# Turned rows of the routing reused by the shared layers, from SBUF or by way of DRAM

## The chip, the cores and the metric

The kernel runs on one core of a Trainium2 chip. Its time is the device time of an execution in microseconds; of several runs the median counts, and of a range the lowest and the highest are given. One further execution is profiled; from it come the trace and all times of single instructions. PE is the matmul engine, PEld its loading of the stationary operand, DVE, ACT and POOL are the vector, scalar and GpSimd engines, and SP is the engine that issues most transfers. Each of them runs its own instructions in order.

## The reference

The input is x, 16 batches of 128 tokens with 256 features in float32, and a context of the same shape. Four layers follow each other, each with a layer normalisation `ln` in front and a gate behind:

```python
x = x + tanh(g_xattn[0]) * long_conv(ctx, ctx, ln(x))
x = x + tanh(g_ffn[0]) * (shared_swiglu(ln(x)) + experts8_top2(ln(x)))
x = x + tanh(g_xattn[1]) * causal_attention16(ln(x), ctx, ctx)
x = x + tanh(g_ffn[1]) * (shared_relu2(ln(x)) + experts32_top6(ln(x)))
```

Both mixtures of experts have a router, which picks 2 of 8 or 6 of 32 experts for every token, and a shared layer, which every token passes. The router and the shared layer of one mixture take the same normalised rows. The shared layer has 1024 hidden units with `silu(g) * u` in the first mixture and 256 with squared ReLU in the second.

## The kernel before, in words

**Tiles.** x stays in SBUF as 16 tiles `xs[b]` of 128 tokens by 256 features, to which every layer adds its part. The layers work on chunks of batches: `CHUNKS` is (0,4), (4,8), (8,12), (12,14), (14,16), and the routing of the second mixture on `GROUPS` (0,4), (4,8), (8,12), (12,14), (14,15), (15,16). A matmul needs its rows with the features on the partitions. So the rows of a chunk are normalised and turned: `stats` (L161 to L182) gives mean and reciprocal deviation, and `turned` (L189 to L208) normalises each tile on DVE (L202), transposes its two halves on PE into a PSUM bank (L205) and copies the bank, two tiles at a time, into a tile `xT` on ACT (L207). In a profile all uses of it share these lines and differ by the names: tp_f and row for the routing, tp_s and xn_s for the shared layers, tp_at and xn_at for the attention. Tiles `xT` come from a ring of four (tag "xT", bufs=4), the PSUM banks for transposes ("tr") from a ring of two.

**First mixture.** `sends0(i)` (L701) does the routing of one half of the batches: norm (statistics, the rows as they are to be sent, and their transposes), choose (logits lg_r at L382, then the selection on DVE), place (each row's place in its expert's list) and the sends (L716), indirect DMAs on POOL that scatter rows into a DRAM buffer. `tiles0` (L736 to L793) reads them back by tiles of 128 rows of one expert (the loads `got`, L747), multiplies, and stores the results `parts`; `combine0` gathers them. `shared0(c)` (L630 to L683) is the shared layer of chunk c as a list of steps: turn, eight times hidden(j) with the matmuls pg and pu (L608, in `up`) and hs (L424), with back(j) (os, L660) one step behind, and add.

**Second half.** `attend` (L814 to L904) is the attention of one batch in five steps, with keys and values loaded by SP (L822, L823). `dispatch(g)` (L934 to L980) is the routing of a group for the second mixture with norm, choose, place and sends (L963); its masks are mb (L550), its positions pos (L555 to L559), its destinations dst (L600). `shared1` (L907 to L930) is the shared layer of a group: turn, two matmul steps p (L608) and o_sh (L616). The expert stage then reads all sent rows (`got`, L1161), turns them (xt, L1175), and runs through 114 tiles of experts.

**What sets the order.** Steps are closures in lists. `woven` (L1012) spreads several lists evenly against each other. `with_sums0` (L1028) makes the list of a chunk's shared layer that is woven with the attention. For the last batches the order is written out by hand (L1063 to L1080), and `some(n)` takes the next n steps of `shared1` there. A scheduler then moves instructions of each engine within what dependencies allow, so that the order of an engine can differ from that of the program. SP's transfers take turns on eight hardware semaphores.

**Where the same rows are turned twice.** The routing's norm in `sends0` and `dispatch` keeps mean and deviation (`keep=True`); `shared0` and `shared1` use them later to normalise and turn the same rows of x again, by `chunk_T` (L369) or `turned`:

```python
        def turn():
            got["xT"] = chunk_T(c, "s0", norm=norm)
...
        def turn():
            got["xT"] = xT = work.tile([P, KC, TOK], F32, tag="xT", name=f"xTs_{g}", bufs=4)
            turned(work, list(range(b0, b1)), mv, rs, columns(xT, b1 - b0), f"s1{g}")
```

Of the kernel before, what the change touches and what calls it, by code (L numbers as in the profile page):

```python
# [10 lines left out]
F32 = mybir.dt.float32  # L11
# [7 lines left out]
P = 128  # L19
B = 16  # L20
D = 256
KC = D // P
# [10 lines left out]
WARM = 22  # L33

E0, SH0, TOPK0 = 8, 8, 2
PARTS0 = [(0, 8), (8, 16)]
NT0 = 8 * TOPK0 + E0 - 1
W0_ROW = 3 * D
# [15 lines left out]
def flamingo(ctx: ExitStack, tc: tile.TileContext, a: dict, out: bass.AP):  # L54
# [154 lines left out]
    def columns(xT, n):  # L209
        return lambda j: xT[:, :, 2 * j * P : min(2 * j + 2, n) * P].rearrange("p c (k t) -> p k c t", t=P)  # L210
# [158 lines left out]
    def chunk_T(c, label, scale=1.0, norm=None):  # L369
        xT = work.tile([P, KC, TOK], F32, tag="xT", name=f"xT_{label}{c}", bufs=4)  # L370
        tiles = list(range(*CHUNKS[c]))
        mv, rs = norm or stats(tiles, f"{label}{c}")
        turned(work, tiles, mv, rs, columns(xT, len(tiles)), f"{label}{c}", scale=scale)
        return xT


    def router(xT, n, rw, ne, label):

# [248 lines left out]

        return [[(b - b0, b) for b in range(i, min(i + 2, b1))] for i in range(b0, b1, 2)]

    def shared0(c, norm):  # L630

        b0, b1 = CHUNKS[c]
        n = (b1 - b0) * P
        tiles = pairs(b0, b1)
        got, hs = {}, [None] * SH0

        def turn():
            got["xT"] = chunk_T(c, "s0", norm=norm)

        def hidden(j):  # L640
            cols = slice(j * P, (j + 1) * P)
            p1 = up(lambda kc: wB[:, kc, 0, cols], got["xT"], n, f"pg_{c}_{j}")
            p2 = up(lambda kc: wB[:, kc, 1, cols], got["xT"], n, f"pu_{c}_{j}")
            hs[j] = work.tile([P, TOK], F32, tag="h", name=f"hs{c}_{j}", bufs=3)[:, :n]
            silu_gate(p1, p2, hs[j], n, f"{c}_{j}")

        def back(j):
            if j == 0:
                got["o"] = [bank("so", f"os{c}_{i}", 2) for i in range(len(tiles))]
                for o in got["o"]:  # L650
                    T.matmul(
                        o.rearrange("p (h t) -> p h t", t=P),
                        lhsT=zeros_b,
                        rhs=ident_b.unsqueeze(1).to_broadcast([P, 4, P]),
                        start=True,
                        stop=False,
                    )
            for o, ts in zip(got["o"], tiles):
                for k, (t, _) in enumerate(ts):
                    T.matmul(  # L660
                        o[:, k * D : (k + 1) * D],
                        lhsT=hs[j][:, t * P : (t + 1) * P],
                        rhs=wC[:, j, :],
                        start=False,
                        stop=(j == SH0 - 1 and k == len(ts) - 1),
                    )

        def add():
            for o, ts in zip(got["o"], tiles):
                for k, (_, b) in enumerate(ts):  # L670
                    V.scalar_tensor_tensor(xs[b], o[:, k * D : (k + 1) * D], tg_h, xs[b], ALU.mult, ALU.add)

        def step(j):
            if j < SH0:
                hidden(j)
            if j > 0:
                back(j - 1)

        return [turn] + [lambda j=j: step(j) for j in range(SH0 + 1)] + [add]
# [4 lines left out]
            follow(ins, other, reason)  # L684


    norms0 = {}

    def sends0(i):

        b0, b1 = PARTS0[i]
        chunks = [c for c in range(len(CHUNKS)) if b0 <= CHUNKS[c][0] < b1]
        got = {}
        scatters = []

        def norm(c):
            n = CHUNKS[c][1] - CHUNKS[c][0]
            tiles = list(range(*CHUNKS[c]))
            rows = [work.tile([P, ROW], F32, tag="row", name=f"row0_{b}", bufs=8) for b in tiles]
            got.setdefault("rows", []).extend(rows)  # L700
            got["xT"] = xT = work.tile([P, KC, TOK], F32, tag="xT", name=f"xT_f0{c}", bufs=4)  # L701
            norms0[c] = stats(tiles, f"f0{c}", keep=True)
            turned(work, tiles, *norms0[c], columns(xT, n), f"f0{c}", keep=lambda k: rows[k][:, :D])

        def choose(c):
            if c == chunks[0]:
                got["masks"] = small.tile([P, HALF, E0], BF16, tag="masks0", name=f"masks0_{i}", bufs=1)
                got["eqs"] = small.tile([P, HALF, TOPK0, E0], F32, tag="eqs0", name=f"eqs0_{i}", bufs=1)
            choose0(got["xT"], c, got["masks"], got["eqs"])

        def place():
            got["table"] = place0(i, got["masks"], got["eqs"])

        def send(t):
            for k in range(TOPK0):
                ins = G.indirect_dma_start(  # L716
                    out=sent0[i][:, :],
                    out_offset=bass.IndirectOffsetOnAxis(ap=places0[:, b0 + t, k : k + 1], axis=0),
                    in_=got["rows"][t][:, :D],
                    in_offset=None,  # L720
                )
                for other in scatters:
                    tc.declare_no_dep(ins.ins, other.ins, reason="no two of the rows sent share a place")
                scatters.append(ins)
                if k == 0:
                    paced(ins)

        steps = []
        for c in chunks:
            steps += [lambda c=c: norm(c), lambda c=c: choose(c)]  # L730
        return steps + [place] + [lambda t=t: send(t) for t in range(b1 - b0)], got, scatters
# [172 lines left out]
        return [lambda: scores(0), lambda: scores(1), turn, values, add]  # L904


    def shared1(mv, rs, g):  # L907

        b0, b1 = GROUPS[g]
        n = (b1 - b0) * P  # L910
        got, hs = {}, []

        def turn():
            got["xT"] = xT = work.tile([P, KC, TOK], F32, tag="xT", name=f"xTs_{g}", bufs=4)
            turned(work, list(range(b0, b1)), mv, rs, columns(xT, b1 - b0), f"s1{g}")

        def hidden(j):
            ps = up(lambda kc: ws[:, j, kc * P : (kc + 1) * P], got["xT"], n, f"p1_{g}_{j}")
            r = work.tile([P, TOK], F32, tag="act", name=f"relu_{g}_{j}", bufs=4)[:, :n]
            S.activation(r, ps, AF.Relu)  # L920
            h = work.tile([P, TOK], F32, tag="h", name=f"h1_{g}_{j}", bufs=3)[:, :n]
            S.activation(h, r, AF.Square)
            hs.append(h)

        def back(i, ts):
            down(hs, [ws[:, j, KC * P :] for j in range(SH1)], lambda t: tg_f[:, 1:2], ts, f"sh{g}_{i}")

        return (
            [turn]
            + [lambda j=j: hidden(j) for j in range(SH1)]  # L930
            + [lambda i=i, ts=ts: back(i, ts) for i, ts in enumerate(pairs(b0, b1))]
        )
# [3 lines left out]
    def dispatch(g):  # L936
# [5 lines left out]
        def norm():  # L942
            got["rows"] = rows = [
                work.tile([P, ROW], F32, tag="row", name=f"row{b}", bufs=8) for b in range(b0, b1)
            ]
            got["xT"] = xT = work.tile([P, KC, TOK], F32, tag="xT", name=f"xT1_{g}", bufs=4)
            tiles = list(range(b0, b1))
            got["norm"] = stats(tiles, f"f1{g}", keep=True)
            turned(work, tiles, *got["norm"], columns(xT, n), f"f1{g}", keep=lambda k: rows[k][:, :D])

        def choose():
            got["chosen"] = choose1(got["xT"], g)
# [23 lines left out]
        sends = []  # L976
        for t in range(n):
            sends += [lambda t=t: send(t), *wait[1:]]
        shares[g] = lambda: shared1(*got["norm"], g)
        return [norm, *wait[1:], choose, *wait, place, *sends]  # L980

    aT, begun = {}, {}
# [32 lines left out]
    def woven(*lists):  # L1015

        at = [((i + 0.5) / len(l), k, step) for k, l in enumerate(lists) for i, step in enumerate(l)]
        for _, _, step in sorted(at, key=lambda x: x[:2]):
            step()
# [5 lines left out]
    def sums0(c):  # L1025
        return [lambda b=b: combine0(b) for b in range(*CHUNKS[c])]

    def with_sums0(c):  # L1028

        steps = shared0(c, norms0[c])  # L1030
        for k, add in enumerate(sums0(c)):
            steps[3 + k] = lambda now=steps[3 + k], add=add: (now(), add())
        return steps + [nothing, lambda: begin(c), nothing]
# [2 lines left out]
    sendB, gotB, scatB = sends0(1)  # L1036
    for step in sendA[:2]:
        step()
    woven(shared0(0, norms0[0]), sendA[2:] + [nothing] * 2)
    more = shared0(1, norms0[1])  # L1040
    woven(tiles0(0, gotA, scatA, "sc"), [nothing] * 3 + sendB + [nothing] * 6, more[:5])
    woven(sums0(0), more[5:8])
    begin(0)
    beside = [
        lambda: more[8:-1] + [lambda: (more[-1](), [step() for step in sums0(1)])] + tiles0(1, gotB, scatB)
        + [lambda: begin(1), nothing],
        lambda: with_sums0(2),
        lambda: with_sums0(3) + [lambda: load_w1(12, W0_END // W1_ROW)],
# [254 lines left out]
```

## Time and profile before

| | us |
|---|---|
| three runs | 849.39, 840.36, 846.49 |
| their median | 846.49 |
| the profiled execution's own time | 845.23 |
| its span in the trace | 843.5 |
| PE busy, mean granted clock 0.908 | 726.8 |
| DVE busy | 539.7 |
| ACT busy | 367.8 |
| POOL busy | 332.7 |

By time, the span falls into these stages: the long convolution to 112 us, the first mixture's routing to about 172, its experts and shared layers to 350 (beside the first batches' attention from 270), attention with the last shared layers of the first mixture and the routing of the second to 643, the expert stage of the second mixture to 808, and the gathering and output to 843.5.

The profile's lines give an instruction's line in the kernel, its engine and operation, the tile that it writes and those that it reads (written `out<-in`), its shape, and how often it occurs. In a timeline the first two numbers are start and duration in us, and a bracket tells how long the engine sat idle before and which engine, operation and line released it. The granted clock is the share of the full clock that PE was given.

### The profile page before, as it was taken

The numbers are of one execution on the slowest core, as the hardware profiler recorded it, in microseconds if no ns is written. First come the engines' busy times: TensorE is split into PE (matmuls) and PEld (weight loads), VectorE is DVE, ScalarE is ACT, GpSimd is POOL, SyncE is SP. The second block draws the span as 40 slices with busy tenths as digits, with TensorE's granted clock in tenths as the row PEclk, the third lists the DMA queues.
The fourth block names the chain that finished last, engine by engine and source line by source line (L and its number), as shares of the span: only waits on it lengthen the run. The fifth ranks groups of instructions, "written<-read, shape, count | busy, mean of one in ns | idle before, by whom it ended". The sixth has DMA issues, their size and how long they took to land.

```text
span 843.5 us, 12155 instructions
## 1 busy us (share of the span) xinstructions
PE 726.8 (86%) x3928; PEld 506.5 (60%) x3928; DVE 539.7 (64%) x1579; ACT 367.8 (44%) x811; POOL 332.7 (39%) x326
## 2 busy tenths in 40 slices
PE   6999979989999999999989989689776999688930
PEld 3444454567675687665658657556445898677820
DVE  5999995337336855568757955666783554465755
ACT  2010036024423766642365355236424777556724
POOL 3766603200607000012561074037252677665750
PEclk8999978999999999999989979959877999889975
DMA  8999996122433243711232143333125666787575
GB/s 265 325 366 261 276 252 173 44 88 76 170 106 103 49 125 93 189 32 35 84 103 44 15 126 81 109 93 112 40 86 189 207 223 209 238 276 238 191 240 184
DMA packets 134016, 128.97 MB, mean 153 GB/s; under 512 B 42976, under 2 KB 117888, under 8 KB 133824
## 3 DMA queue, kind: packets, MB, share of 16 engines
q1 hardware_dynamic: 120704, 91.61, 38.9%
q0 software_dynamic: 13152, 36.52, 12.1%
q8 instruction: 32, 0.52, 0.3%
q14 instruction: 32, 0.26, 0.1%
q10 hardware_dynamic: 96, 0.05, 0.0%
HBM read 64.23 MB, written 63.92 MB: 152 GB/s over the span
## 4 chain that ended last, share of the span: by engine, by line
PE 53%; DVE 19%; DMA 8%; issue 7%; ACT 7%; POOL 3%; ACTq 1%; SPq 0%; DVEq 0%; POOLq 0%
PE y L330 7%; PE sc L846 5%; PE gu L773 4%; PE eo L1194 4%; PE pg L608 4%; PE pu L608 3%; PE eh L1182 3%; PE pt L867 3%; PE os L660 3%; PE eo L783 3%; DMA part<-parts 2%; DMA parts<-ey,to 2%; PE avT L881 2%; PE p L608 2%; ACT ex L860 2%
## 5 line engine op out<-in xcount | busy, mean ns | idle before, releaser
L963 POOL DMA_INDIRECT sent<-row,dst x96 | 93.4, 973 | 136.7 <-DVE dst L600 104.4
L1219 POOL DMA_INDIRECT parts<-ey,to x114 | 112.1, 984 | 62.4 <-ACT ey L1203 31.1
L860 ACT ACTIVATE ex<-sc,mn 128x128 f32<-128x128 f32 x256 | 71.7, 380 | 51.2 <-DVE mn L854 51.1
L803 POOL DMA_INDIRECT part<-parts,places x32 | 31.0, 970 | 142.4 <-DVE rd L897 86.1
L330 PE MATMUL y<-kv,toe 128*128 128x512 f32 x192 | 84.9, 597 | 0.0
L1194 PE MATMUL eo<-wt,ehs 128*128 128x256 f32 x228 | 63.7, 412 | 21.3 <-DVE ehs L1192 21.1
L322 POOL TENSOR_TENSOR kv<-cT 128x1024 f32<-128x1024 f32 x32 | 60.5, 1892 | 37.9 <-PE y L330 33.0
L1172 ACT COPY wt<-wts 128x512 f32 x114 | 66.3, 620 | 13.0 <-issue 8.3
L716 POOL DMA_INDIRECT sent<-row,places x32 | 31.2, 975 | 103.3 <-DVE places L495 38.0
L608 PE MATMUL pg<-xT_s,wts 128*128 128x512 f32 (+1 forms) x160 | 68.1, 548 | 0.4 <-DVE silu L423 0.4
L1182 PEld LDWEIGHTS eh<-xts,wt 128*128 128x128 f32 x456 | 62.2, 201 | 7.2 <-ACT wt L1172 3.6
L1182 PE MATMUL eh<-xts,wt 128*128 128x128 f32 x456 | 64.7, 286 | 1.6 <-ACT wt L1172 1.5
L608 PE MATMUL pu<-xT_s,wts 128*128 128x512 f32 (+1 forms) x160 | 64.0, 520 | 2.1 <-DVE hs L424 2.1
L660 PE MATMUL os<-wts,hs 128*128 128x256 f32 x256 | 64.2, 386 | 0.0
L846 PE MATMUL sc<-keys,xT_at 32*128 32x256 f32 x256 | 61.0, 441 | 0.0
L330 PEld LDWEIGHTS y<-kv,toe 128*128 128x128 f32 x192 | 35.9, 191 | 41.2 <-issue 29.1
L1194 PEld LDWEIGHTS eo<-wt,ehs 128*128 128x128 f32 x228 | 41.8, 201 | 29.3 <-DVE ehs L1192 24.5
L660 PEld LDWEIGHTS os<-wts,hs 128*128 128x128 f32 x256 | 48.3, 193 | 15.6 <-issue 9.7
L1177 DVE COPY xts<-xt 128x512 f32<-128x512 f32 x57 | 38.6, 685 | 29.2 <-PE xt L1175 21.6
L854 DVE TENSOR_REDUCE mn<-sc 128x4 f32<-128x512 f32 x64 | 42.3, 682 | 15.8 <-PE sc L846 15.5
L1203 ACT COPY ey<-eo 128x512 f32<-128x512 f32 x57 | 33.4, 585 | 40.0 <-PE eo L1194 39.8
L773 PEld LDWEIGHTS gu<-xts,wt 128*128 128x128 f32 x368 | 46.3, 196 | 7.1 <-issue 2.5
(250 smaller groups left out, 1379.9 us busy)
## 6 DMA issues: line engine op xcount, KB each, us to landing
sent<-keys SPq DMA_DIRECT2D x1, 17018.0 KB
got<-sent SPq DMA_DIRECT2D x19, 804.0 KB, 5.1
part<-parts SPq DMA_DIRECT2D x48, 256.0 KB, 3.8
sent<-keys SPq DMA_DIRECT2D x2, 2944.0 KB
got<-sent SPq DMA_DIRECT2D x22, 256.0 KB, 2.8
parts<-ey SPq DMA_DIRECT2D x22, 256.0 KB, 2.6
wts<-in_sw SPq DMA_DIRECT2D x3, 1024.0 KB, 10.2
wts<-in_w SPq DMA_DIRECT2D x3, 1024.0 KB
```

The source lines that it names most:

```text
L322: G.tensor_tensor(kv, c[:, :, hs].unsqueeze(3).to_broadcast(full), c[:, :, hs].unsqueeze(2).to_broadcast(full), ALU.mult)
L330: T.matmul(y[:, lb * TOK : (lb + 1) * TOK], lhsT=t[:, off : off + P], rhs=kv[:, kc * HALF : (kc + 1) * HALF].rearrange("p b i j -> p (b i ...
L608: T.matmul(ps, lhsT=w(kc), rhs=xT[:, kc, :n], start=(kc == 0), stop=(kc == KC - 1))
L660: T.matmul(o[:, k * D : (k + 1) * D], lhsT=hs[j][:, t * P : (t + 1) * P], rhs=wC[:, j, :], start=False, stop=(j == SH0 - 1 and k == len(ts ...
L773: T.matmul(gu[:, half * D + u * P : half * D + (u + 1) * P], lhsT=wt[:, u, w : w + P], rhs=xt[:, u * D + kc * P : u * D + (kc + 1) * P], s ...
L846: T.matmul(scs[r][:, kc * D : (kc + 1) * D], lhsT=xT[rows, kc, cols], rhs=kz[rows, kc].rearrange("p m t -> p (m t)"), start=False, stop=(k ...
L860: S.activation(ex[:, i, :], scs[r][:, at : at + P], AF.Exp, bias=mn[:, i : i + 1], scale=-1.0)
L963: ins = G.indirect_dma_start(out=sent[:, :], out_offset=bass.IndirectOffsetOnAxis(ap=dst[:, t, k : k + 1], axis=0), in_=row, in_offset=None,)
L1172: S.copy(wt[:, i], wts[:, bass.ds(offsets[u % GRP], W1_ROW)])
L1182: T.matmul(eh[:, i * P : (i + 1) * P], lhsT=wt[:, i, cols], rhs=xt[:, i * D + kc * P : i * D + (kc + 1) * P], start=(kc == 0), stop=(kc == ...
L1194: T.matmul(eo[:, i * D : (i + 1) * D], lhsT=h[:, i * P : (i + 1) * P], rhs=wt[:, i, KC * P :], start=True, stop=True,)
L1219: ins = G.indirect_dma_start(out=parts[:, :], out_offset=bass.IndirectOffsetOnAxis(ap=to[:, t % GRP : t % GRP + 1], axis=0), in_=y[:, t % ...
```

## The change

The routing's turned rows are kept, and the shared layers take those. For chunks 0 and 1 of the first mixture (`HERE = 2`), the tile `xT` of the routing itself is used. For chunks 2 to 4 and all six groups of the second mixture, `put` stores the tile to a DRAM tile after the norm step, and `again` takes a fresh tile of the ring and loads it back in the shared layer's turn step. `stats` is then called without `keep`, so that mean and deviation lie in small rotating tiles. `put` and `again` issue their DMAs on SP. In the main order, step hidden(7) of chunk 1's shared layer now stands ahead of `begin(0)`, the attention's own turned rows of chunk 0, which take a tile of the same ring. Nothing else is changed in the program; the scheduler's order of some other instructions moves with it.

```diff
+HERE = 2
...
+    def put(xT, n, label):
+
+        kept = dram.tile([P, KC, n], F32, tag=f"kept_{label}", name=f"kept_{label}")
+        nc.sync.dma_start(out=kept, in_=xT[:, :, :n])
+        return kept
+
+    def again(kept, n, label):
+        xT = work.tile([P, KC, TOK], F32, tag="xT", name=f"xT_{label}", bufs=4)
+        nc.sync.dma_start(out=xT[:, :, :n], in_=kept)
+        return xT
...
-    def shared0(c, norm):
+    def shared0(c):
...
-            got["xT"] = chunk_T(c, "s0", norm=norm)
+            got["xT"] = turned0[c] if c < HERE else again(turned0[c], n, f"s0{c}")
...
-            norms0[c] = stats(tiles, f"f0{c}", keep=True)
-            turned(work, tiles, *norms0[c], columns(xT, n), f"f0{c}", keep=lambda k: rows[k][:, :D])
+            turned(work, tiles, *stats(tiles, f"f0{c}"), columns(xT, n), f"f0{c}", keep=lambda k: rows[k][:, :D])
+            turned0[c] = xT if c < HERE else put(xT, n * P, f"f0{c}")
...
-    def shared1(mv, rs, g):
+    def shared1(kept, g):
...
-            got["xT"] = xT = work.tile([P, KC, TOK], F32, tag="xT", name=f"xTs_{g}", bufs=4)
-            turned(work, list(range(b0, b1)), mv, rs, columns(xT, b1 - b0), f"s1{g}")
+            got["xT"] = again(kept, n, f"s1{g}")
...
-            got["norm"] = stats(tiles, f"f1{g}", keep=True)
-            turned(work, tiles, *got["norm"], columns(xT, n), f"f1{g}", keep=lambda k: rows[k][:, :D])
+            turned(work, tiles, *stats(tiles, f"f1{g}"), columns(xT, n), f"f1{g}", keep=lambda k: rows[k][:, :D])
+            got["kept"] = put(xT, n * P, f"f1{g}")
...
-        shares[g] = lambda: shared1(*got["norm"], g)
+        shares[g] = lambda: shared1(got["kept"], g)
...
-    woven(shared0(0, norms0[0]), sendA[2:] + [nothing] * 2)
-    more = shared0(1, norms0[1])
+    woven(shared0(0), sendA[2:] + [nothing] * 2)
+    more = shared0(1)
     woven(tiles0(0, gotA, scatA, "sc"), [nothing] * 3 + sendB + [nothing] * 6, more[:5])
-    woven(sums0(0), more[5:8])
+    woven(sums0(0), more[5:9])
     begin(0)
     beside = [
-        lambda: more[8:-1] + [lambda: (more[-1](), [step() for step in sums0(1)])] + tiles0(1, gotB, scatB)
+        lambda: more[9:-1] + [lambda: (more[-1](), [step() for step in sums0(1)])] + tiles0(1, gotB, scatB)
```

## The prediction

> **What bounds the kernel now.** I read the page's busy row and chain first, then a table of busy time by stage, and then the matmul engine's timeline at the stages that the edits touch.
>
> ```profile
> PE 726.8 (86%) x3928; PEld 506.5 (60%) x3928; DVE 539.7 (64%) x1579; ACT 367.8 (44%) x811; POOL 332.7 (39%) x326
> ...
> PE 53%; DVE 19%; DMA 8%; issue 7%; ACT 7%; POOL 3%; ACTq 1%; SPq 0%; DVEq 0%; POOLq 0%
> ```
>
> PE has 86% of the span and 53% of the chain that ended last, so a PE instruction taken out is worth something wherever PE has no idle time. The stages (columns: us, then busy time of PE, PEld, DVE, ACT, POOL, then granted clock, DMA share, GB/s):
>
> ```profile
> 172.00:270.00 98.00, 92.19 (x486) 67.98 (x486) 49.42 (x173) 34.93 (x61) 29.71 (x31) 0.98 0.34 110
> 270.00:350.00 80.00, 77.97 (x558) 58.66 (x554) 48.39 (x110) 54.49 (x133) 2.04 (x3) 1.00 0.38 104
> 350.00:545.00 195.00, 181.50 (x1102) 122.98 (x1102) 132.16 (x426) 85.18 (x227) 62.50 (x64) 0.94 0.28 72
> 545.00:643.00 98.00, 78.30 (x424) 49.96 (x423) 65.97 (x300) 41.57 (x93) 46.65 (x48) 0.77 0.28 90
> ```
>
> From 172 to 545 us PE is 92 to 97% busy: there a removed PE microsecond is a gained one. From 545 to 643 it is 80% busy at a mean clock of 0.77; something else holds it a fifth of the time. This is the last of the attention and the routing of the last batches. The expert stage behind it cannot start until the last row is sent.
>
> **What is removed.** Counting the two instruction orders: 64 transposes tp_s (L205), 32 normalisations xn_s (L202, median 409 ns) and 17 copies xT_s/xTs (L207, about 0.6 us). By stage, tp_s alone (PE, PEld, ACT, clock, DMA share, GB/s):
>
> ```profile
> 112.00:180.00 68.00, 2.40 (x11) 2.06 (x12) 1.06 (x2) 0.85 0.52 136
> 180.00:270.00 90.00, 1.17 (x7) 0.64 (x5) 1.19 (x2) 0.98 0.34 110
> 270.00:350.00 80.00, 1.26 (x8) 0.85 (x8) 0.77 (x2) 1.00 0.38 104
> 350.00:545.00 195.00, 1.77 (x8) 1.13 (x8) 1.67 (x3) 0.94 0.28 72
> 545.00:644.00 99.00, 7.33 (x32) 4.82 (x32) 4.93 (x9) 0.78 0.28 89
> ```
>
> That is 13.9 us of PE, 13 us of DVE (32 × 0.41) and 9.6 us of ACT. Only the PE part and the waits on the other two stand on the chain.
>
> **What is added.** On SP's queue 9 stores and 9 loads, 3 MB each way against the 129 MB that the kernel moves. SP issues them at 0.38 us (its got loads) to 0.55 us (its vals load), 18 × 0.5 = 9 us on an engine that does nothing else but wait. Nothing is added to POOL, whose indirect DMAs stay as they were. The new stores of layer 0 stand in SP's queue behind the ACT copies that fill their rows, which end in the same stage; those of layer 1 wait for the copy xT at norm, and behind them stand key and value loads that run ahead of their use by three batches: 0. The load that comes back is the only new wait on the chain. Its price, by the nearest rows (KB each, median us to landing):
>
> ```profile
> got<-sent SPq DMA_DIRECT2D x19, 804.0 KB, 5.1
> ...
> got<-sent SPq DMA_DIRECT2D x22, 256.0 KB, 2.8
> ```
>
> So 512 KB take an estimated 3.9 us (midway), 256 KB 2.8 us, 128 KB 2 to 2.8. [...]
>
> **Step A, 112 to 180 us (chunks 0 and 1, kept in SBUF): −3.** 2.40 us of tp_s, and PE's wait for ACT xT_s of 0.56, drop out; no load comes in. But PE here first runs at clock 0.50 and goes to 1.00 from 132 us, after the 512-wide matmuls; in the new order the first of these lie between the halves of the routing's transposes. Gains end where the first routed rows come back (got, 176 us), paced by the shared layer's hs_7 and 16 sends of 1.27 us. Bounds: −6 (the clock comes up sooner) to +1 (the choice, 2 to 3 us later in PE's order, delays the sends).
>
> **Step B, 180 to 270: −1.1.** The transposes of chunk 1's rest in a stage without slack.
>
> **Step C, chunk 2 at 347 us: −0.3.** −1.3 of tp_s; but the load of its rows stands on SP right behind a weight load of 768 KB, and in the new order its first pg comes at about 348 instead of 354 us. At the 340 GB/s that the profile shows there, it lands at 348.5 to 349: I charge 1 us, between 0 and 5 (if all the 1.5 MB behind it share the engines).
>
> **Step D, chunks 3 and 4: −1.8.** The 1.77 us of tp_s in 350 to 545. The loads of 256 KB lie behind key loads that wait for earlier scores, with 5 to 7 us of PE work between them and their use, against 2.8: slack 2 to 4 us. Without the cover they cost up to 2 us each.
>
> **Step E, group 0 of the second layer, 564 to 568: −2.2.** Its two packs of 4 transposes, 1.12 and 1.11 us, at half clock:
>
> ```profile
> 548.90 0.18 PE L555 MATMUL pos<-mb,before_me 128*128 128x32 bf16 x1 [5.58 <-DVE mb L550]
> ...
> 564.49 1.12 PE L205 MATMUL tp_s<-ident,xn_s 128*128 128x128 f32 x4
> ...
> 567.12 1.11 PE L205 MATMUL tp_s<-ident,xn_s 128*128 128x128 f32 x4
> ...
> 571.18 2.41 PE L608 MATMUL p<-xTs,ws 128*128 128x512 f32 x4
> ```
>
> PE stood idle for 5.6 us, and the clock was 0.50 in every 4 us slice from 546 to 570 and 1.00 from 574, though PE was 82 to 100% busy in all but the first. So not every work lifts it: the weight loads and 32-row attention matmuls did not, the 512-wide p did. [...] The row decides: it comes back with p. In the new order p_0_0 comes a few matmuls after the previous batch's transposes, at about 559 to 560. Its 512 KB load is issued behind a value load (552.8), so lands at about 557.3: slack 2 us, hidden. If p then lifts the clock at some 563, the 8 us of half-clock work behind it take 4 less; if the load is late by 3 us, +3. I take −2.2, bounds −6 to +4.
>
> **Step F, group 1, 585 to 600: −5.** 8 tp_s between 589.6 and 593.2 with waits of 0.7 to 1.2 us, then p_1_0, and only then pos of group 3 at 595.75, though its masks mb were ready at 594.4; its other p matmuls (2.57 us from 597.98) stand ahead of group 4's transposes at 600.39. In the new order both p come before pos, in PE's wait for mb. So pos starts at about 593.5 (two xn_s of 0.41 us are also out of DVE's way): −2.3; and p is gone from behind it: −2.6. Bounds −6 to 0 (the place chain on DVE sets the time anyway).
>
> **Step G, group 2, 612 to 620: −5.** The last batch's routing waits on PE:
>
> ```profile
> 612.80 0.45 PE L205 MATMUL tp_f<-ident,row 128*128 128x128 f32 x2 [2.00 <-DVE gw L523]
> 613.05 1.91 PE L205 MATMUL tp_s<-ident,xn_s 128*128 128x128 f32 x8
> 615.64 3.78 PE L608 MATMUL p<-xTs,ws 128*128 128x512 f32 x4 [0.69 <-ACT xTs L207]
> ...
> 619.34 0.85 PE L382 MATMUL lg_r<-rw,xT 128*128 128x32 f32 x4
> ```
>
> Between tp_f of the last batch and its logits lie 1.91 + 0.69 + 3.78 = 6.4 us of another group's work. In the new order the transposes are gone and p follows the logits, which then only wait for ACT's copy, 1.3 us: −5. From there the DVE chain (masks 629.0, dst 634.0) and six sends of 1.27 us remain. Four xn_s (1.6 us) fewer lie on DVE: −1. The sends before them end at 631.6 and then move with group 2's, so POOL does not take over. In F and G the loads for groups 1 to 5 have 3 us and more between the landing and the use.
>
> **Expert stage and end, 643 to 843.5: +3.** Its instructions are the same, but a few transposes and transfers swap places on PE and SP. A sign cannot be told; bounds −3 to +5. I charge +3, also for idle stretches in F and G now empty of matmuls, in which the clock may fall.
>
> **Sum.** −3 −1.1 −0.3 −1.8 −2.2 −5 −5 −1 +3 = −16.4. Against the profiled execution, 845.23 us (span 843.5 and 1.7 around it): 828.8. The runs' median, 846.49, is 1.3 above it: 830.1, say **830**.
>
> **Rivals.**
> 1. *Only the instructions themselves.* The tail is not PE's: its ends are set by the DVE chains of choose and place and by 1.27 us sends, so F and G give only their DVE part. For it: PE is idle for a fifth of 545 to 643; between logits and masks DVE takes 9 us each time. Against: the 6.4 us in G are PE's in plain view. A + B + C + D + E + 1 of DVE = −9.4, +3: about 840.
> 2. *Slower: the clock in the tail.* One mechanism: PE, in order, comes to p of a group before its load; it idles over 3.5 us, the clock falls to 0.50 as at 546, and since the p matmuls are no longer spread over the tail, nothing lifts it. The work done from 572 to 643 is 50.6 us at full clock (busy 57.3 weighted by the clocks of its slices, 0.77 to 1.00); each microsecond of it at half clock costs one more. From 16 us of it on there is no gain; half of it, 25 us, gives 855. For it: 25 us at 0.50 in this very trace. Against: the loads have slack by my count.
> 3. *The transfers wait more, nothing else.* Each of the four tight loads (C, D twice, E) late by 3 us: +12 instead of +1, 841.
> 4. *The clock comes back sooner in A and E,* −7 more: 823.
>
> **How the numbers follow.** About what a measurement of this kernel tells from no change is 1%, 8.5 us, so 838 to 855 is "within". The forecast has 0.50 (its own range 823 to 838), rival 1 has 0.17, rival 3 0.08, rival 4 0.10, rival 2 0.15. Faster by over 1%: 0.50 × 0.93 + 0.10 + 0.05 of rivals 1 and 3 = 0.62. Slower by over 1%: half of rival 2 and more as its price is open, 0.12. The rest is 0.26. The range: 820 below (rival 4 with a little more), 852 above (into rival 2).
>
> **What would show it.** A: got before 174 us. C: PE's wait before pg with a DMA as releaser; over 1 us says that the load is late. E: the clock is 1.00 before 570; p waits for a DMA if I am wrong. F and G: no p between mb and pos, lg_r within 2 us of tp_f, the last six sends starting at about 618 where they started at 634. If the sends start less than 8 us sooner, rival 1 holds; if the clock row shows 5 or 6 in the tail, rival 2; if the expert stage is longer than 200 us from the first got to the end, the swaps cost more than I charged.

## The result and the profile after

The changed kernel takes 832.78 us (median of four runs, 829.81 to 833.36), against 844.3 for the kernel before in the same comparison. The ratio is 0.9855, with a 95% interval of 0.9808 to 0.9903: some 12 us or 1.5% faster. The forecast was 830, some 16 us below the 846.49 that then stood for the kernel before. Total and direction fit; the steps by which they came about fit only in part, and that is what the experiments are about. Medians in this document are of all runs of a kernel; its ratios leave out runs that lay over 1.5% above the kernel's fastest, as did two of the six runs behind the 823.36 us below, the profiled one among them.

The page of the changed kernel, its span and busy row:

```profile
span 831.3 us, 11987 instructions
...
PE 707.3 (85%) x3864; PEld 494.5 (59%) x3864; DVE 530.2 (64%) x1547; ACT 356.9 (43%) x792; POOL 332.7 (40%) x326
```

The 64 transposes are gone (3928 to 3864 matmuls). PE lost 19.5 us of busy time though the transposes had only 13.9; that the others ran at a mean granted clock of 0.916 instead of 0.908 goes with the rest. Busy time by stage, as before (PE, PEld, DVE, ACT, POOL, granted clock, DMA share, GB/s); the stages are the same stretches of time, so their work has moved forward a little:

```profile
172.00:270.00 98.00, 90.79 (x477) 66.90 (x477) 48.65 (x171) 34.37 (x61) 30.81 (x32) 0.98 0.39 123
270.00:350.00 80.00, 75.24 (x518) 57.17 (x516) 42.50 (x96) 51.29 (x122) 0.00 (x0) 0.94 0.33 92
350.00:545.00 195.00, 180.08 (x1107) 122.07 (x1107) 135.60 (x441) 85.64 (x232) 62.59 (x64) 0.94 0.34 91
545.00:643.00 98.00, 72.48 (x410) 49.36 (x410) 61.80 (x277) 40.07 (x89) 46.81 (x48) 0.78 0.44 139
```

The second row stands out. In a stage that had a clock of 1.00 it is now 0.94, and 40 matmuls fewer got done, of which 8 are transposes that are gone. To see where the time went, I set the same events of the two traces side by side (us from the span's start):

| event | before | after | lead |
|---|---|---|---|
| first routed rows read (got) | 176.17 | 172.48 | 3.7 |
| last gather of chunk 1 (part) | 271.82 | 268.39 | 3.4 |
| first gather of chunk 2 (part) | 358.92 | 360.68 | −1.8 |
| destinations dst, group 1 | 483.29 | 482.95 | 0.3 |
| dst, group 2 | 559.01 | 555.30 | 3.7 |
| dst, group 3 | 603.77 | 593.68 | 10.1 |
| dst, group 5 (the last) | 633.68 | 624.45 | 9.2 |
| first rows of the expert stage read | 643.35 | 633.79 | 9.6 |
| end of the span | 843.5 | 831.3 | 12.2 |

The lead of step A is lost between 268 and 361 us. It is won again between groups 1 and 3, and between groups 3 and 5 nothing is added, although the forecast had its largest term there. The experiments look at these two places, at the two halves of the change, and at the transfers.

### The profile page after: what moved, and what is told of

The parts are those of the page before. It is cut to its first block, busy times and chain, and to the rows that moved or that the text cites. A ratio compares the mean times of both kernels' runs of the same rounds, so it can differ in the third digit from the quotient of the medians.

```text
span 831.3 us, 11987 instructions
## 1 busy us (share of the span) xinstructions
PE 707.3 (85%) x3864; PEld 494.5 (59%) x3864; DVE 530.2 (64%) x1547; ACT 356.9 (43%) x792; POOL 332.7 (40%) x326
## 3 DMA queue, kind: packets, MB, share of 16 engines
q0 software_dynamic: 13152, 36.52, 12.2%
## 5 line engine op out<-in xcount | busy, mean ns | idle before, releaser
L1193 PEld LDWEIGHTS eh<-xts,wt 128*128 128x128 f32 x456 | 59.8, 196 | 5.2 <-issue 1.2
L1193 PE MATMUL eh<-xts,wt 128*128 128x128 f32 x456 | 62.3, 281 | 0.1
L331 PEld LDWEIGHTS y<-kv,toe 128*128 128x128 f32 x192 | 35.8, 191 | 41.2 <-issue 29.1
L858 PE MATMUL sc<-keys,xT_at 32*128 32x256 f32 x256 | 59.1, 437 | 0.0
L785 PEld LDWEIGHTS gu<-xts,wt 128*128 128x128 f32 x368 | 48.8, 203 | 8.2 <-DVE xts L779 3.6
L785 PE MATMUL gu<-xts,wt 128*128 128x128 f32 x368 | 51.8, 290 | 0.4 <-DVE xts L779 0.3
L434 ACT ACTIVATE silu<-pg 128x512 f32<-128x512 f32 (+1 forms) x40 | 21.0, 525 | 65.4 <-PE pg L620 65.2
```

Of the source, the lines that this page charges most:

```text
L331: T.matmul(y[:, lb * TOK : (lb + 1) * TOK], lhsT=t[:, off : off + P], rhs=kv[:, kc * HALF : (kc + 1) * HALF].rearrange("p b i j -> p (b i ...
L785: T.matmul(gu[:, half * D + u * P : half * D + (u + 1) * P], lhsT=wt[:, u, w : w + P], rhs=xt[:, u * D + kc * P : u * D + (kc + 1) * P], s ...
L858: T.matmul(scs[r][:, kc * D : (kc + 1) * D], lhsT=xT[rows, kc, cols], rhs=kz[rows, kc].rearrange("p m t -> p (m t)"), start=False, stop=(k ...
L1193: T.matmul(eh[:, i * P : (i + 1) * P], lhsT=wt[:, i, cols], rhs=xt[:, i * D + kc * P : i * D + (kc + 1) * P], start=(kc == 0), stop=(kc == ...
```

## The experiments

The runs were made on three chips, each beside the kernel before on the same chip. On the second chip every kernel took some 14% longer, the kernel before too (959.96 us): in a trace of the changed kernel there (after_again), PE stood still 11 times for more than 4 us, 90 us in all, where the first trace has 3 times and 24 us. From that chip only ratios and what a single stage shows are used.

**The two halves.** In the first kernel the second mixture turns its rows again, in the second the first mixture does:

```diff
 # l0only
-            got["xT"] = again(kept, n, f"s1{g}")
+            got["xT"] = xT = work.tile([P, KC, TOK], F32, tag="xT", name=f"xTs_{g}", bufs=4)
+            turned(work, list(range(b0, b1)), *kept, columns(xT, b1 - b0), f"s1{g}")
...
 # l1only: shared0, sends0 and the main order as before; shared1 and dispatch as changed
```

> The change in the first mixture alone (chunks 0 to 4); the second mixture normalises and turns its rows again as before. My theory: A brings its 3.7 us, but shifting the shared step hidden(7) lets the expert tiles start earlier in the weave, PE waits on DVE near 278 us and runs 10 us at half clock, which costs about 5: nothing is left by the first sends of the second mixture, and the whole is 844 us, within 3 of the kernel before. The reckoning of the prediction, which saw no such loss, says 6.2 less: 838.

> The change in the second mixture alone (six groups by way of DRAM); the first mixture as before, its order too. My theory: all of the gain comes from here. The last destinations dst come about 8 us earlier than before, got likewise, and the whole is 835 us, give or take 3 for swaps in the expert stage. If the two halves shared the gain as the prediction's sums say (6.2 from the first mixture, 10 net from the second), it is 836 here too, but then the run of the first mixture alone must show 838.

Measured: the first mixture alone 840.14 us, ratio 0.9961 (0.9937 to 0.9986), which lies between the two numbers expected; the second alone 834.52, ratio 0.9903 (0.987 to 0.9937), as expected. So most of the gain comes from the second mixture, and the first one's is about 3 us where the prediction's sums had 6.2. In the trace of the second mixture alone, the last dst is at 624.21, as in the changed kernel (624.45); the stages before 545 us are those of the kernel before to within 1 us.

**First theory for the loss after 268 us: the weave.** The list woven with the first attention batches is one step shorter since hidden(7) left it, so the expert tiles stand earlier; PE waited there 1.5 us for a copy of theirs (DVE xts). I put an empty step in:

```diff
-        lambda: more[9:-1] + [lambda: (more[-1](), [step() for step in sums0(1)])] + tiles0(1, gotB, scatB)
+        lambda: [nothing] + more[9:-1] + [lambda: (more[-1](), [step() for step in sums0(1)])] + tiles0(1, gotB, scatB)
```

> The changed kernel with one empty step at the front of the list that is woven with batches 0 to 3 of the attention, so that the expert tiles stand where they stood in the kernel before. My theory: the half-clock stretch at 279 to 289 us is gone, its 5 us come back, 828 us. Rival, that the loss between 180 and 360 us is the load of chunk 2 or the stores on SP: the clock may change but parts of the third chunk are no earlier, and it stays at 833.

Measured: 834.33 us, ratio 0.9889 (0.9851 to 0.9927), no better than the changed kernel, where 828 was expected. The wait for xts was gone, and the clock fell all the same, in the middle of the four scores of the second line:

```profile
282.42 0.38 PE L848 MATMUL sc<-causal_b,ident_b 128*128 128x512 bf16 x1 [0.58 <-ACT ex L872]
282.72 1.41 PE L858 MATMUL sc<-keys,xT_at 32*128 32x256 f32 x4
```

The interval from the last gather of chunk 1 to the first of chunk 2 was 90.4 us, where the kernel before has 87.1. As the cause of the fall, this theory fell.

**Second theory: the moved step itself.** With hidden(7) ahead of begin(0), the os matmuls of back(6), which belong to the same step, are done before the attention's first scores instead of among them. (The pg and pu of hidden(7) run ahead of the scores in both orders.) Two kernels test it. One is the kernel before with only this move; the other is the changed kernel with `HERE = 1`: chunk 1 goes by way of DRAM as well, its slot of the ring comes free, and the step can stay where it was.

```diff
 # step_moved_only, on the kernel before
-    woven(sums0(0), more[5:8])
+    woven(sums0(0), more[5:9])
     begin(0)
     beside = [
-        lambda: more[8:-1] + [lambda
+        lambda: more[9:-1] + [lambda
...
 # one_from_sbuf, on the changed kernel
-HERE = 2
+HERE = 1
...
-    woven(sums0(0), more[5:9])
+    woven(sums0(0), more[5:8])
     begin(0)
     beside = [
-        lambda: more[9:-1] + [lambda
+        lambda: more[8:-1] + [lambda
```

> The kernel before with one thing of the change: step hidden(7) of chunk 1's shared layer ahead of begin(0). No transpose is removed. Second theory (os matmuls missing among the first scores): the interval from the last gather of chunk 1 to the first of chunk 2, 87.1 us in the kernel before, becomes 90.5 to 92.5, with clock 0.50 for 8 to 10 us near 280; the whole is 3 to 5 us slower than before. Rival (chance of the clock's window, or the stores): interval 87, same time as before.

> HERE = 1: chunk 1 too goes by way of DRAM, which leaves its slot of the ring free, so that step hidden(7) can stay behind the start of the attention, as in the kernel before; PE's order is that of before, less the transposes, up to chunk 2. My second theory for the loss before 360 us: it is this step's dense matmuls os, missing between the first scores of the attention (32 rows high), that let the clock fall. Then the clock at 274 to 294 us is 1.00, parts of the third chunk (358.9 before, 360.7 after) come at about 355, and the time is 828. Rival, that the clock falls there by chance of its window in any of these kernels: the stretch of half clock is there again, 833. A third, that the load of chunk 1 comes late in a stage without slack: a wait of pg for a DMA near 200 us and over 833.

> The changed kernel itself, a second profile. If the fall of the clock near 280 us belongs to its order, it is there again; its time is 833. If it was chance, the clock is 1.00 there and the third chunk's parts come at 355 to 356 us.

> HERE = 1 and the step left in place, again, since all four kernels of the last call ran 14 per cent longer on their chip, the kernel before too. By the second theory the interval is 87 us and the time 828 where the changed kernel has 833; by the rival 833.

> The changed kernel itself as the reference of this call: 833, interval 90.5 to 92.5 us, expert stage (first rows read to the end) 197 us give or take 2.

Measured: the move alone makes the kernel before slower, 847.75 against 840.64 us, ratio 1.0077 (1.0049 to 1.0104): 6 to 7 us, more than the 3 to 5 expected. Without the move the change brings 823.36 us, ratio 0.977 (0.9734 to 0.9806), beside 833.22 and 0.9891 (0.9856 to 0.9926) for the changed kernel on the same chip. On the slower second chip the ratios were 0.9828 (0.9781 to 0.9874) without the move and 0.9948 (0.9924 to 0.9971) with it. The interval in all profiles (us), and how much of it the clock took, estimated as half of the time at 0.50 in it (in step_moved_only four scores take 1.13 us at 1.00 and two take 1.22 at 0.50):

| step hidden(7) | kernels | interval | of it, by the clock |
|---|---|---|---|
| in place | before, l1only, one_from_sbuf, one_from_sbuf_hold, one_from_sbuf_2, one_from_sbuf_hold_2 | 87.1, 87.1, 86.5, 86.8, 84.5, 84.5 | 0, 0, 1.0, 1.3, 0, 0 |
| moved | after, after_again, after_third, l0only, weave_as_before, hold_shared, step_moved_only, load_twice | 92.3, 94.9, 94.5, 90.5, 90.4, 90.7, 94.3, 97.6 | 5.1, 7.9, 8.5, 3.4, 6.8, 3.4, 5.1, 7.9 |

No kernel of the second row comes near the first, so it is not chance. (The 1.0 and 1.3 of the first row, on the second chip, are from a fall in a stop of PE of some 4 us, ahead of the scores; a part of after_again's and load_twice's is too.) With the step in place and the transposes gone the interval is 84.5 on the third chip, 2.6 less than before. With it moved, after, l0only and hold_shared come to 87.1 to 87.3 without the clock's part, of which 1.5 us are the wait for xts; weave_as_before, without that wait, comes to 83.6. So by this estimate the clock took 3.4 to 8.5 us, and it is the larger part of what the move costs. PE's timeline of the kernel before with the move alone, where the scores begin:

```profile
273.28 1.13 PE L846 MATMUL sc<-keys,xT_at 32*128 32x256 f32 x8
274.34 1.56 PE L660 MATMUL os<-wts,hs 128*128 128x256 f32 x6
...
278.04 1.13 PE L846 MATMUL sc<-keys,xT_at 32*128 32x256 f32 x4
...
281.50 1.13 PE L846 MATMUL sc<-keys,xT_at 32*128 32x256 f32 x4
284.10 0.59 PE L836 MATMUL sc<-causal_b,ident_b 128*128 128x512 bf16 x1 [1.48 <-DVE xts L767]
...
285.47 1.22 PE L846 MATMUL sc<-keys,xT_at 32*128 32x256 f32 x2
```

Behind the six os there are only scores of 32 rows, the causal mask's matmuls (bf16), short transposes and small waits up to the fall at 283.4, for 7.5 us. The kernel before has two packs of os among its scores:

```profile
270.46 1.99 PE L660 MATMUL os<-wts,hs 128*128 128x256 f32 x8
...
275.22 1.56 PE L660 MATMUL os<-wts,hs 128*128 128x256 f32 x6
...
278.93 1.09 PE L867 MATMUL pt<-ident,ex 128*128 128x128 f32 x8
...
283.28 1.09 PE L867 MATMUL pt<-ident,ex 128*128 128x128 f32 x8
...
287.02 2.05 PE L773 MATMUL gu<-xts,wt 128*128 128x128 f32 x16
```

The clock of that kernel (columns as above, the clock is the third number from the end):

```profile
278.00:282.00 4.00, 4.00 (x19) 2.60 (x19) 4.00 (x10) 2.28 (x8) 0.00 (x0) 1.00 0.32 82
282.00:286.00 4.00, 2.52 (x9) 1.62 (x9) 4.00 (x10) 3.09 (x10) 0.00 (x0) 0.67 0.07 18
286.00:290.00 4.00, 4.00 (x13) 2.29 (x12) 1.13 (x6) 3.31 (x4) 0.00 (x0) 0.50 0.00 0
290.00:294.00 4.00, 4.00 (x19) 3.69 (x19) 0.78 (x2) 0.58 (x2) 0.00 (x0) 0.55 0.00 0
```

and of the one with `HERE = 1` and the step in place (with the held matmuls of the next experiment, which lie far behind):

```profile
278.00:282.00 4.00, 3.83 (x18) 2.27 (x17) 4.00 (x9) 2.57 (x8) 0.00 (x0) 1.00 0.08 23
282.00:286.00 4.00, 3.43 (x24) 2.67 (x25) 3.49 (x13) 4.00 (x11) 0.00 (x0) 1.00 0.39 123
286.00:290.00 4.00, 4.00 (x56) 3.12 (x55) 2.39 (x7) 3.94 (x7) 0.00 (x0) 1.00 0.35 43
290.00:294.00 4.00, 4.00 (x31) 3.74 (x31) 2.14 (x6) 3.55 (x7) 0.00 (x0) 1.00 0.48 132
```

In the first, four scores take 1.13 us ahead of the fall and two take 1.22 us behind it; in the second the clock never leaves 1.00. That the move costs time is shown, most of it by the clock as estimated above, and weave_as_before shows that the fall does not need the 1.5 us wait. That it is the lack of os is not shown: behind its last pack the kernel before, too, has only scores, masks and transposes from 276.8 us until gu begins at 287.0, and its clock stays at 1.00.

The traces differ in something finer. In each of them all changes of the granted clock lie whole multiples of 3.413 us apart; the half-clock stretches there in the moved kernels, outside the second chip, lasted 6.83 to 17.07 us, 2 to 5 times that. In all eight moved kernels the last 3.413 us ahead of the fall among the scores hold at most 0.44 us of os and float32 transposes. Every other such stretch at full clock between the first score and the expert tiles' gu, in these and in the kernels with the step in place, holds 0.58 us or more. So transposes may do as well as os; no run has put either alone into the gap.

**The held matmuls: where step G went.** PE's timeline of the changed kernel at the last group's routing:

```profile
603.17 0.41 PE L206 MATMUL tp_f<-ident,row 128*128 128x128 f32 x2 [1.98 <-DVE gw L535]
606.69 0.19 PE L567 MATMUL pos<-mb,before_me 128*128 128x32 bf16 x1 [3.10 <-DVE gates L550]
...
606.75 1.04 PE L394 MATMUL lg_r<-rw,xT 128*128 128x32 f32 x4
...
607.65 6.34 PE L620 MATMUL p<-xT_s,ws 128*128 128x512 f32 x8
613.83 1.03 PE L628 MATMUL o_sh<-ws,h 128*128 128x256 f32 x4
614.69 0.59 PE L620 MATMUL p<-xT_s,ws 128*128 128x256 f32 x2
615.34 2.86 PE L628 MATMUL o_sh<-ws,h 128*128 128x256 f32 x12
618.04 0.18 PE L567 MATMUL pos<-mb,before_me 128*128 128x32 bf16 x1
```

The logits no longer wait for p, but for the pos of the group before, which stands ahead of them in PE's order and waits 3.10 us for its own inputs: they come 3.6 us after tp_f instead of 6.5, not the 1.3 of the forecast. And both p of group 2, with their o_sh, now stand between these logits and the last pos. The last masks mb were ready at 615.4; pos came at 618.04. Behind it, DVE has the sums of the shared layer in its chain to dst:

```profile
618.24 0.88 DVE L636 SCALAR_TENSOR_TENSOR x<-o_sh,g_ffn,x 128x256 f32<-128x256 f32 x2 [0.42 <-PE pos L571]
619.03 0.18 DVE L578 TENSOR_SCALAR up_i<-pos 128x32 int32<-128x32 f32 x1
...
622.20 0.48 DVE L636 SCALAR_TENSOR_TENSOR x<-o_sh,g_ffn,x 128x256 f32<-128x256 f32 x1 [0.27 <-PE o_sh L628]
...
624.45 0.17 DVE L612 CAST dst<-dstf 128x6 uint32<-128x6 f32 x1
```

From mb (615.21) to dst it is 9.2 us, where the kernel before had 4.8. So I made the p of groups 2 to 5 wait for the last pos:

```diff
-    def up(w, xT, n, name):
+    def up(w, xT, n, name, behind=None):
...
+            if kc == 0 and behind is not None:
+                follow(ins, behind, "it is not needed before")
...
-            ps = up(lambda kc: ws[:, j, kc * P : (kc + 1) * P], got["xT"], n, f"p1_{g}_{j}")
+            ps = up(lambda kc: ws[:, j, kc * P : (kc + 1) * P], got["xT"], n, f"p1_{g}_{j}", state["pos"] if g >= 2 else None)
...
-        some(1), at(15, 4), send3[0], choose4, norm5, some(3), send3[1], place4, send4, choose5, some(4), place5, send5,
+        some(1), at(15, 4), send3[0], choose4, norm5, some(3), send3[1], place4, send4, choose5, place5, send5,
```

> The changed kernel, with the matmuls p of groups 2 to 5 made to wait for the last group's pos, so that they run while its rows are sent. Same work. My theory: the new wait of step G is these matmuls in front of pos; pos then comes with its masks, 2.7 us earlier, the DVE chain behind it is free of the shared layers' sums, dst comes 4 us earlier, and the time is 829 us. Rival, that DVE's own chain is the bound: dst at most 1 us earlier, 832 to 833; and if the held matmuls run past the arrival of the first rows, it is slower.

> The last one with the matmuls p of groups 2 to 5 held behind the last pos. If both causes are right and add up, 824; if only the second is, 829 as for hold_shared.

> Both remedies, again: 824 if they add up (833 less 5 for the clock and 4 to 6 for the sends, of which a part is lost in the expert stage), 829 if only the held matmuls work.

PE's timeline of hold_shared:

```profile
605.34 1.04 PE L394 MATMUL lg_r<-rw,xT 128*128 128x32 f32 x4
...
614.02 0.21 PE L567 MATMUL pos<-mb,before_me 128*128 128x32 bf16 x1 [7.62 <-DVE mb L562]
...
614.25 6.30 PE L620 MATMUL p<-xT_s,ws 128*128 128x512 f32 x8
...
632.20 0.30 PE L1188 MATMUL xt<-ident,got 128*128 128x128 f32 x1 [0.17 <-DMA got<-sent]
```

Now pos comes with its masks, and dst 4.35 us behind them: at 618.14 instead of 624.45, and the first rows of the expert stage are read at 627.53 instead of 633.79. From dst of group 2 to that of group 5 it is 63.0 us in both profiled kernels with the hold outside the second chip, 66.7 to 69.2 in those that have the second mixture's change without it. So the stall of G is shown, and that it was removed. The time says less: 828.97 us as expected, ratio 0.9849 (0.9817 to 0.9881), hardly apart from the changed kernel's 0.9855 and 0.9891; and with `HERE = 1`, 824.73 with the hold and 823.36 without (0.9777 and 0.977). On the second chip it was 0.9798 (0.9755 to 0.9841) with, 0.9828 without. Of the 6 us that the traces show at 627 us, the ratios with `HERE = 2` show 0.5 to 3.5 us, which their intervals do not tell from nothing; with `HERE = 1` they show none on the third chip. The hold leaves PE idle for 7.6 us before the p, runs them below the full clock (6.30 us for eight; in the changed kernel, at 0.50 up to 613.02, eight took 6.34, and the six from 557.59, at 0.95 to 1.00, took 3.15) and lets them end with the first xt at 632.20, where the changed kernel's PE is idle for 12 us (from 626.36). That this eats the gain is argued only; where it goes in the runs that were not profiled stays open.

**The transfers.** Every load of kept rows was issued twice, the second waiting for the first:

```diff
         nc.sync.dma_start(out=xT[:, :, :n], in_=kept)
+        nc.sync.dma_start(out=xT[:, :, :n], in_=kept)
```

> The changed kernel with every load of kept rows issued twice into the same tile, the second when the first has landed, so that the rows come some 3 to 4 us later at nine places. Theory that the loads are hidden with slack: PE waits for a DMA before pg or p at no more than one or two places, at most 4 us in all: 833 to 838. Rival, that the loads are on the path already: 3 us at four or more places, 845 and above.

Measured, on the second chip: ratio 1.008 (1.0043 to 1.0116) beside the changed kernel's 0.9948 there, about 1.3% slower, twice what I expected at most. All waits for kept rows in its trace (total us, times, longest):

```profile
PEld p L621 <- DMA xT_s<-kept_f: 3.6, 1, 3.6
PE p L621 <- DMA xT_s<-kept_f: 3.5, 1, 3.5
PEld pg L621 <- DMA xT_s<-kept_f: 1.7, 1, 1.7
PE pg L621 <- DMA xT_s<-kept_f: 1.5, 1, 1.5
```

That is 5 us on PE at two of nine places. In the trace of the changed kernel, and of every other one with single loads, there is no wait of this kind at all. So the loads are hidden, and at seven places with more slack than a second load takes. The other 8 us or so of the slowdown are not waits for rows; the scheduler also made another order of it, and I cannot divide them.

A single load was dearer than the prediction had it. The traces tell the landing of two loads of 512 KB of kept rows: 5.3 us (one_from_sbuf_2, issued at 565.99) and 6.2 us (l1only, at 566.77), against the 3.9 estimated from the rows of other loads. In the changed kernel the two tightest loads of that size were issued 5.7 and 6.3 us before their use, so their cover was thin.

## Why the prediction was right, point by point

| step | forecast | measured in the profiled pair | |
|---|---|---|---|
| A | −3 | −3.7 | inside its bounds |
| B, C, D | −3.2 | +3.4 | wrong sign: the moved step |
| E | −2.2 | −3.4 | inside its bounds |
| F | −5 | −6.4 | a little over |
| G with DVE's 1 | −6 | +0.9 | wrong: a new wait |
| expert stage and end | +3 | −3.0 | wrong sign, inside its bounds |
| sum | −16.4 | −12.2 | |

The pair is one execution on each side. The same stretches in all profiles but those of the second chip (us):

| stretch | in the order before | as changed |
|---|---|---|
| first got (A) | 176.2, 176.0, 177.8 | 171.9 to 177.5 |
| first got to dst of group 1 (B, C, D) | 307.1, 307.1 | step in place 306.3, 306.6; moved 309.5 to 314.1 |
| dst of group 1 to group 3 (E, F) | 120.5, 115.2, 115.7 | 110.7 to 112.6 |
| dst of group 3 to group 5 (G) | 29.9, 29.1, 29.0 | 28.3 to 30.8; held 24.5, 24.5 |
| last dst to the end | 209.8, 204.3, 204.9 | 205.0 to 210.6 |

The first number of a row is the kernel before; the others are l1only and step_moved_only for A, l1only for B to D, and l0only and step_moved_only below, whose steps there are those of the kernel before. (step_moved_only moved the step without the change: 313.4 in the second row.) So the pair flatters E and F, which are worth some 3 to 5 us beside the other two profiles and not 9.8, and what it shows for G and for the end lies within what executions differ by.

**A.** The logits and first shared matmuls ran at the full clock in this profile (the first 16 lg_r in 1.95 us, the first four pg in 1.88). In the kernel before only the first 16 lg_r did (1.95); what differs is the stretch from 120 to 132 us, at 1.00 here and at 0.50 to 0.69 there, where the next 16 lg_r took 3.59 us and the first four pg 3.76. In others with the same order the lg_r ran at half (3.58 us in l0only). Over the profiles that have the change here, the first got lies between 171.9 and 177.5 us, with the old order between 176.0 and 177.8. So A is worth about 2 us in the mean. How much in one execution seems to be the clock's doing; no run tests it.

**B, C, D.** The transposes are gone and no load is waited for, as forecast, though of the forecast 3.2 us only 0.5 to 0.9 are found where the step stays in place. What was missing is a term. The sum prices the transposes taken out and the loads put in, and has no price for hidden(7), which the change moves past the start of the attention. It cost 5.2 us in the profiled pair (92.3 against 87.1 us), and 6 to 7 us alone. PE's idle time does not tell it either: PE was never idle for more than 1.5 us there, and for no more than 0.6 us in weave_as_before. A row in the prediction, in step E, pointed to it: from 550 to 570 us PE was 82 to 100% busy with weight loads, 32-row scores and transposes, and the clock stayed at 0.50.

**E.** As forecast, the clock comes back near the start of p, and earlier than before. Busy times of the changed kernel in slices (clock third from the end):

```profile
554.00:558.00 4.00, 4.00 (x17) 3.09 (x18) 3.54 (x8) 2.32 (x7) 1.75 (x2) 0.50 0.44 159
558.00:562.00 4.00, 4.00 (x18) 1.89 (x16) 1.95 (x5) 1.18 (x5) 3.08 (x4) 0.95 0.28 103
562.00:566.00 4.00, 4.00 (x46) 2.17 (x46) 1.29 (x2) 2.37 (x10) 2.98 (x4) 1.00 0.41 113
```

The first p starts at 557.59, its load was issued at 551.91, and no wait lies between. I took the transposes' 2.2 us and left 4 more as a bound; it was 3.4 in the pair. That p is what lifts the clock, as I read it from one trace, does not hold. In l0only and step_moved_only the clock is back at 570.3 and 576.9, 0.2 us ahead of their first p, behind a pack of avT. PE and clock of l0only:

```profile
568.80 1.77 PE L893 MATMUL avT<-pT,vals 128*32 128x128 f32 x32
570.50 1.98 PE L620 MATMUL p<-xTs,ws 128*128 128x512 f32 x4
...
566.00:570.00 4.00, 4.00 (x34) 2.34 (x36) 2.01 (x4) 0.97 (x3) 3.08 (x4) 0.50 0.33 119
570.00:574.00 4.00, 4.00 (x32) 2.27 (x26) 0.94 (x4) 3.51 (x10) 3.08 (x4) 0.97 0.62 136
```

Counted from dst of group 1, the clock does come back 7 to 13 us earlier in every profile with the change outside the second chip; which instructions bring it back stays open.

**F.** The place chain from mb to dst of group 3 took 7.2 instead of 9.5 us. That looks like the 2.3 forecast to the digit, but it is the clock of one execution: in l0only and step_moved_only, with p in the same place ahead of pos, the chain took 6.8. In the kernel before (the first two lines) these p ran at a clock of 0.50, in l0only (the last two) at 1.00:

```profile
593.88 2.08 PE L608 MATMUL p<-xTs,ws 128*128 128x512 f32 x2 [0.69 <-ACT xTs L207]
595.75 0.23 PE L555 MATMUL pos<-mb,before_me 128*128 128x32 bf16 x1
...
592.53 1.13 PE L620 MATMUL p<-xTs,ws 128*128 128x512 f32 x2 [0.69 <-ACT xTs L208]
593.49 0.18 PE L567 MATMUL pos<-mb,before_me 128*128 128x32 bf16 x1
```

What stays is gained ahead of the masks: from dst of group 2 to mb of group 3 it is 31.1 to 32.5 us with the change and 34.7 to 35.3 without, which fits the earlier clock of E, though no run tests that. F came out by another way than the forecast's.

**G.** The step that failed. "In the new order the transposes are gone and p follows the logits, which then only wait for ACT's copy" is half true: they wait for pos of the group before. And I looked at what p no longer delays and not at what it delays now. Behind the logits it stands ahead of the last pos, and its sums stand in DVE's chain. The 6.4 us of work that it set out to take away were dear in that execution besides: from 613 to 620 us its clock was at 0.50.

**Expert stage.** From the first rows read to the end it took 200.2 us before and 197.5 after, 201.2 with the change in the second mixture alone, and 194.7 to 197.8 in the seven other profiles outside the second chip, two of which have the old order in the second mixture (194.7 and 195.5). Its instructions are the same everywhere, and no effect of the change is seen: the order's swaps, or chance, are worth 3 us and more either way. That the pair's 3.0 offset half of G is luck.

**The rivals.** The third (transfers) is out: no waits. The second (the clock in the tail) is there in part, 0.50 from 589 to 599 and from 606 to 613, but the tail is still shorter. Of stops of PE like that rival's, over 3.5 us, the kernel before has six, 3.62 to 6.75 us long, each with a fall of the clock to 0.50 in it or at most 1.1 us behind it; its falls at 121.5, 377.5 and 592.6 us have no stop of over 1.5 us in the 12 us ahead of them. The first (tail bound by DVE) is nearest for G. In the pair the total came out near the forecast because A, E, F and the end were better by some 9 us and B to D and G worse by some 13. That these nearly cancel is luck: two of the steps failed, and of the larger gains one came by another way and one by chance of the execution.

## What to carry to other kernels

When a step is moved to free a buffer, price what it leaves behind: here 2 us of os matmuls taken from among the scores cost 6 to 7 us, the larger part by the clock (an estimated 5.1 of 7.2 us in step_moved_only), as much as half of what the whole change brought. When work is moved behind one instruction of a critical chain, look for the next instruction of that chain on the same engine, and on the engine that finishes the work. Compare more than one profile on each side before a term of the sum is called confirmed: steps E and F and the end differ by 5 us between executions of the same order. A round trip through DRAM instead of recomputing cost no wait here where a load of 512 KB was issued some 6 us before its use, and it keeps buffers, and with them the order, as they were: sending one more chunk through DRAM was the best version measured, 823.36 us.

## What the runs showed of the hardware that was not expected

The clock fell to 0.50 with PE busy 90 to 100% of each slice around it, when for 8 us only 32-row scores, bf16 mask matmuls, 128-column transposes and waits of at most 0.6 us ran (weave_as_before, fall at 283.44); with one more pack of os among the scores it stayed at 1.00 (the kernel before, 276 to 294 us). In each trace all changes of the granted clock lie on one grid of 3.413 us; against the start of the span it lies elsewhere from one execution to another (from 0.06 us behind it in step_moved_only to 3.16 in one_from_sbuf_2). One chip ran the kernel before in 959.96 us where the others had 841 to 844, with PE's long stops adding up to 90 us in after_again, against 24 us in the first trace of the changed kernel.
